# A capacity expert layer inside a scan stage: its steps moved off VectorE and to other slots

## The chip, the cores and the metric

The kernel runs on one core of a Trainium2 chip. A core has five engines, each with its own in-order queue: TensorE (PE; its weight loads are listed as PEld), VectorE (DVE), ScalarE (ACT), GpSimd (POOL) and SyncE (SP), which here only issues transfers. Engines wait for one another by semaphores. The metric is the device time of one execution in microseconds (us); a kernel is judged by the median of several executions.

## The reference

Two blocks are applied to x (32 sequences of 256 tokens of 128 numbers), all in float32. Each block is an attention-like part and a feed-forward part, both with layer norms whose scale, shift and gate come from a small vector per sequence.

- Block 0: an attention over 16 heads of 8, then a mixture of 8 experts of which each token takes 2.
- Block 1, first part: a layer norm, then a Mamba scan forwards and backwards over the tokens (256 channels, 16 states), a norm, and a Fourier layer (sines and cosines of 8 multiples, with a matrix for each).
- Block 1, second part: a mixture of 8 experts in which a token goes to its best expert alone, and each expert takes only its first 80 tokens over the whole batch:

```
expert_idx = argmax(softmax(tokens @ gate_w + gate_b))
pos  = place of the token among those of its expert;  keep = pos < 80
h    = gelu(dispatch @ w1 + b1)                 # 80 x 512 for each expert
out  = (h @ w2 + b2) * gate_prob                # back to the tokens kept
x    = x + gb * out
```

So the last part writes at most 640 of the 8192 rows. The kernel finds them in the first 16 sequences, and only if some expert has not filled its 80 places by then does a branch at the end look at the rest; with these inputs it isn't taken.

## The kernel before

**Stages.** Block 0 runs first, for some 1,450 us. Then comes the scan stage, written in one loop over *units*. A sequence (a "batch" in this text) is 16 units; there are 512. A unit is 1,024 columns of states: PE spreads two vectors over the state rows (`spread_out`, L1447: `arg` and `ub`, both in PSUM), ScalarE takes the exponential (`decay`, L1453), VectorE multiplies `ub` by B (`by_b`, L1464) and scans (`scanned`, L1471), GpSimd multiplies the scan's result by C (`by_c`, L1484), PE sums over the states of two units at once (`gathered`, L1503), and VectorE gates every fourth result (`gate_y`, L1532).

**The order is written by hand.** The loop issues, for iteration g: the spreads of `arg` for unit g+2 and `ub` for g+1, the exponential of g+2, the scan of g, the side steps of slot g, the sum over units g−3 and g−2 (if g is odd), the product by B of g+1, the product by C of g, the gate, and the side steps of slot g+0.5. On PE, ScalarE, VectorE and GpSimd this is the order of the queues. SP's transfers are ordered by when their data and buffers are expected to be ready. `arg` has one PSUM buffer, `ub` two, the scan's result six.

**Side steps** are generators that advance at listed slots, counted from the first unit of their batch. `front(b)` prepares batch b (slots −39 to −3.5: norms, input projections, convolution, the exponential and logarithm of the time steps; its transfers include the load of B and C, `bc`). `gate(b)` takes a silu at −9.5. `back(b)` does the output projection, a norm and the Fourier layer at slots 19 to 44, and for the first 16 batches also the norm ahead of the experts (`last_norm`, 45.5 to 54), which stores the rows, the gates and the shares that the experts read (`fin_d`). Every eight batches `choose` ranks the tokens. In slot p of a batch, steps of three or four batches come together: slot 6.5, say, has the second pair of sines of `back` and the silu of `gate`, slot 3 the first pair and the silu of `front`, slot 12 GpSimd's sums for x, on which VectorE's statistics in slot 12.5 wait.

**One bank.** All side products on PE write one PSUM bank, `m`. A side step that uses it has to wait until the step before has been read.

**Tables.** ScalarE loads a table set before it takes another kind of function. `table(which)` loads it if another is in, and `steps` loads the exponential's set at the end of every call, so after every slot g and every slot g+0.5.

**The experts** of the last part (`expert`, called by `first_places`) run as one stream, one after another, from batch 19 on, each with its weights (`weights_of`: w1, w2, b2, which is broadcast over 128 partitions). Expert e starts in slot 6 of batch 19+e:

- slot 6: the weights' loads, and a gather of the ranks of its places (L1011, an indirect transfer issued by GpSimd)
- 8.5: VectorE compares the ranks with the places (L1022), sums (L1023), and makes the row's number, once as it is for the later scatter (`to_u`) and once limited for the gather (`of_u`; L1024 to L1029)
- 10: the gather of 80 rows of `fin_d` (L1032)
- 13.5: PE transposes them (L1040), VectorE copies the transpose (`dT`, L1042) and multiplies the gate row by the share (L1044)
- 1.5 of the next batch: PE's first product (L1049), gelu on ScalarE (L1055)
- 3.5: PE's second product (L1061), and on VectorE the bias, the product with the gate row, and the sum with x (L1063 to L1065)
- 6: the scatter to the output (L1069)

Each of these tiles has one buffer.

Of the kernel before, what the change touches and what calls it, by code (L numbers as in the profile page):

```python
# [71 lines left out]
def body(ctx: ExitStack, tc: tile.TileContext, a: dict, out: bass.AP):  # L72
# [90 lines left out]
    def over_e(v, n):  # L163
        return v.unsqueeze(2).to_broadcast([P, n, E])
# [737 lines left out]
    chosen = route.tile([P, E, n_t], F32, tag="chosen", name="chosen")  # L902
    rt = pool(ctx, "d_rt")

    def choose(c, bank):

        n = LAST
        restart("d")
        pr = wide(rt, n)
        nc.vector.tensor_tensor(  # L910
            pr[:], lg[:, c % 2 * n : (c % 2 + 1) * n, :], gate_b[:].unsqueeze(1).to_broadcast([P, n, E]), ALU.add
        )
        top = thin(rt, n)
        nc.vector.tensor_reduce(top[:], pr[:], AX.X, ALU.max)
        nc.vector.tensor_tensor(pr[:], pr[:], over_e(top[:], n), ALU.subtract)
        nc.scalar.activation(pr[:], pr[:], AF.Exp)
# [88 lines left out]
        nc.vector.tensor_tensor(at[:], at[:], iota_e[:], ALU.add)  # L1005
        nc.vector.tensor_copy(at_u[:], at[:])

    def expert(pl, e, w1, w2, b2, bank, po_bank, n, table=None, apart=False):

        counts = pl.tile([P, P], F32, tag="counts_of", name="counts_of")  # L1010
        nc.gpsimd.indirect_dma_start(  # L1011
# [5 lines left out]
        yield  # L1017

        token = pl.tile([P, 1], F32, tag="token", name="token")
        to_u = pl.tile([P, 1], U32, tag="to_u", name="to_u")  # L1020
        of_u = pl.tile([P, 1], U32, tag="of_u", name="of_u")
        nc.vector.tensor_scalar(counts[:CAP], counts[:CAP], place[:CAP], None, ALU.is_le)  # L1022
        nc.vector.tensor_reduce(token[:CAP], counts[:CAP], AX.X, ALU.add)  # L1023
        nc.vector.scalar_tensor_tensor(  # L1024
            token[:CAP], in_tile[:CAP, e : e + 1], float(P), token[:CAP], ALU.mult, ALU.add
# [2 lines left out]
        nc.vector.tensor_scalar(token[:CAP], token[:CAP], float(n * P - 1), None, ALU.min)  # L1028
        nc.vector.tensor_copy(of_u[:CAP], token[:CAP])  # L1029
        yield  # L1030
        of = pl.tile([P, FIN], F32, tag="fin", name="fin")[:CAP]
        nc.gpsimd.indirect_dma_start(  # L1032
            out=of,
# [5 lines left out]
        ps = bank()  # L1039
        nc.tensor.transpose(ps[:, :CAP], of[:, 0:D], ident[:CAP, :CAP])  # L1040
        dT = pl.tile([P, CAP], F32, tag="dT", name="dT")
        nc.vector.tensor_copy(dT[:], ps[:, :CAP])  # L1042
        gb = of[:, FIN_G : FIN_G + D]
        nc.vector.tensor_scalar(gb, gb, of[:, FIN_S : FIN_S + 1], None, ALU.mult)  # L1044
        yield
        ph = bank()
        g = pl.tile([P, NF, CAP], F32, tag="g", name="g")
# [8 lines left out]
                g[:, c, :], ph[:, c * P : c * P + CAP], AF.Gelu_apprx_tanh, bias=col("b1", e * NF + c)  # L1056
            )
        yield
        po = po_bank()
        for c in range(NF):  # L1060
            nc.tensor.matmul(po[:CAP, :D], g[:, c, :], w2[:, c, :], start=(c == 0), stop=(c == NF - 1))  # L1061
        y = pl.tile([P, D], F32, tag="y", name="y")[:CAP]
        nc.vector.tensor_tensor(y, po[:CAP, :D], b2[:CAP], ALU.add)  # L1063
        nc.vector.tensor_tensor(y, y, gb, ALU.mult)
        nc.vector.tensor_tensor(y, y, of[:, FIN_X : FIN_X + D], ALU.add)  # L1065
        yield
        if apart:
            nc.gpsimd.memset(apart_of[:], 0.0)
        ins = nc.gpsimd.indirect_dma_start(  # L1069
# [14 lines left out]
    def weights_of(pl, e):  # L1084
# [1 line left out]
        nc.sync.dma_start(w1[:], a["w1_1"][e])  # L1086
        w2 = pl.tile([P, NF, D], F32, tag="w2", name="w2")
        nc.sync.dma_start(w2[:], a["w2_1"][e].rearrange("(c f) d -> f c d", f=P))
        b2 = pl.tile([P, D], F32, tag="b2", name="b2")
        nc.sync.dma_start(b2[:], a["b2"][e].partition_broadcast(P))  # L1090
        return w1, w2, b2

    cont = route.tile([P, E, LAST], F32, tag="cont", name="cont")
# [2 lines left out]
    with ExitStack() as st:  # L1096
# [13 lines left out]
        def bank():  # L1110
            return m_bank
# [24 lines left out]
        def front(b):  # L1136
# [87 lines left out]
            for d in range(2):  # L1224
# [9 lines left out]
                nc.scalar.activation(u[:, d].rearrange("p n t -> p (n t)"), ps[:], AF.Abs)  # L1234
                nc.scalar.activation(dt[:, d].rearrange("p n t -> p (n t)"), ps[:], AF.Relu)
                yield
            nc.scalar.activation(u[:], u[:], AF.Exp, scale=-1.0)
            nc.scalar.activation(u[:], u[:], AF.Ln, bias=1.0)
            yield
# [59 lines left out]
        def back(b, h, ys):  # L1299
# [79 lines left out]
            done = 2 * (b + 1)  # L1379
            if done % LAST == 0:  # L1380
                yield
                yield from choose(done // LAST - 1, bank)
                if b == FIRST - 1:
                    streams.append((b, UNITS * b, first_places(bank), [PLACES_AT] + EXPERTS_AT))

        PLACES_AT = 68
        EXPERTS_AT = [16 * e + at for e in range(4, E + 4) for at in (6, 8.5, 10, 13.5, 17.5, 19.5)]
        EXPERTS_AT.append(16 * (E + 4) + 6)  # L1390


        BACK_AT = (
# [118 lines left out]
        def first_places(bank):  # L1512
# [3 lines left out]
            nc.vector.tensor_reduce(flag[:, 0:1], chosen[0:1, :, n - 1], AX.X, ALU.min)  # L1516
            nc.vector.tensor_scalar(flag[:, 1:2], flag[:, 0:1], float(CAP), None, ALU.is_lt)
            nc.vector.tensor_copy(left[:], flag[:, 1:2])
            yield
            for e in range(E):  # L1520
                yield from expert(few, e, *weights_of(few, e), bank, bank, n, table=table, apart=True)

        gated = {}
        streams = []
# [11 lines left out]
        with tc.manual_schedule(engines=MANUAL):  # L1536
            started = 0

            def steps(at):
                for stream in sorted(streams, key=lambda w: w[0]):  # L1540
                    _, first, work, slots = stream
                    if slots and at == first + slots[0]:
                        slots.pop(0)
                        if next(work, work) is work or not slots:
                            streams.remove(stream)
                if at + 2 < n_u:
                    table(EXP_LN)

            for g in range(FRONT_AT[0], n_u + 6 * UNITS):
# [26 lines left out]
    with tc.If(missing > 0), ExitStack() as st:  # L1576
# [22 lines left out]
                    pass  # L1599
        tile_of_places(wd, n_t)  # L1600
        for e in range(E):
            for _ in expert(sp, e, *weights_of(sp, e), a_bank, a_bank, n_t):
                pass


# [106 lines left out]
```

## Time and profile before

| | |
|---|---|
| median of 5 executions | 3692.46 us (3680.94 to 3700.82) |
| the profiled execution | 3695.73 us, span 3693.9 us |
| first scan starts, last scan ends | 1450.7, 3662.3 us |
| busy: PE, DVE, ACT, POOL | 85%, 71%, 59%, 71% of the span |
| granted PE clock, mean | 0.907 |

"Span" is the time from the first instruction to the last. A group in the profile is all instructions of one line, engine and shape: after the count stand its busy time in us and the mean of one in ns, then the idle time of its engine just before them and what ended it. A line of waits reads: who waited, for whom, us in total, times, the longest. A timeline line has start, duration, engine, source line, operation, and in brackets the idle time before. A line of stretches has, for each stretch of time, its length, then busy us (and instructions) of PE, PEld, DVE, ACT and POOL, the granted clock, the DMA engines' busy share and GB/s. In the slices the span is cut into 40 equal parts, and a digit is the busy share in tenths.

### The profile page before, as it was taken

Reading aid. Unit: us, or ns where it says so; the run is one execution under the profiler, and the core shown is the slowest. Engines: PE = TensorE matmul, PEld = TensorE weight load, DVE = VectorE, ACT = ScalarE, POOL = GpSimd, SP = SyncE. Lnnn points to the kernel's source line nnn. Section 1 sums busy time; section 2 is a strip of 40 time slices with the busy share of each in tenths; the row PEclk is TensorE's granted clock in tenths of the full one; section 3 lists DMA queues with packets and bytes.
Section 4 is the critical chain, followed back from the end, with each engine's and each line's share of the span. In section 5 each row is a group of like instructions: output and inputs, shape, how many; then the busy total and the mean of one; then the engine's idle time right before and its main releaser. Section 6 shows DMA issues by size and latency. Waiting matters only on the chain. (4 is left out here: it accounts for less than half of the span.)

```text
span 3693.9 us, 68522 instructions
## 1 busy us (share of the span) xinstructions
PE 3153.3 (85%) x27356; PEld 2155.2 (58%) x27356; DVE 2621.0 (71%) x3450; ACT 2162.9 (59%) x3242; POOL 2633.4 (71%) x2632
## 2 busy tenths in 40 slices
PE   6989998884999986888889888889888888888886
PEld 3655665552778773555556555556555555555555
DVE  3566666653223223998888888888888888888996
ACT  2666666652223224577676667676666667666775
POOL 4466566555666654888888878888877887778884
PEclk8999999985999996999899889899888899899998
DMA  2630000001222212011121111121111111111100
GB/s 80 266 139 26 24 25 24 26 25 59 91 94 93 67 55 47 21 29 36 32 40 31 32 36 35 33 45 26 32 28 36 34 30 38 38 30 25 28 17 8
DMA packets 133227, 173.73 MB, mean 47 GB/s; under 512 B 26447, under 2 KB 98662, under 8 KB 128676
## 3 DMA queue, kind: packets, MB, share of 16 engines
q1 hardware_dynamic: 105428, 88.13, 10.3%
q0 software_dynamic: 23168, 46.93, 4.0%
q10 hardware_dynamic: 4304, 34.21, 2.3%
q8 instruction: 217, 3.56, 0.4%
q14 instruction: 110, 0.90, 0.1%
HBM read 127.10 MB, written 79.97 MB: 56 GB/s over the span
## 5 line engine op out<-in xcount | busy, mean ns | idle before, releaser
L1484 POOL TENSOR_TENSOR hs<-hs,bc 128x1024 f32<-128x1024 f32 x512 | 1204.8, 2363 | 353.8 <-DVE hs L1471 347.0
L1471 DVE TENSOR_TENSOR_SCAN hs<-da,ub 128x1024 f32<-128x1024 f32 x512 | 1166.5, 2278 | 29.2
L1447 PE MATMUL arg<-dt,spread_a 32*128 32x256 f32 x4096 | 752.9, 436 | 72.8 <-ACT da L1453 71.7
L1453 ACT ACTIVATE da<-arg 128x1020 f32<-128x1020 f32 x512 | 521.7, 1019 | 465.7 <-PE ub L1447 402.3
L1447 PE MATMUL ub<-u,spread 32*128 32x256 f32 x4096 | 652.6, 439 | 92.4 <-DVE hs L1471 45.6
L1464 DVE TENSOR_TENSOR ub<-ub,bc 128x1024 f32<-128x1024 f32 x512 | 620.2, 1211 | 34.6 <-PE ub L1447 34.4
L1447 PEld LDWEIGHTS arg<-dt,spread_a 32*128 32x128 f32 x4096 | 448.8, 201 | 236.9 <-ACT da L1453 126.0
L1447 PEld LDWEIGHTS ub<-u,spread 32*128 32x128 f32 x4096 | 396.5, 204 | 150.8 <-DVE hs L1471 81.0
L578 DVE TENSOR_REDUCE q<-x 128x4 f32<-128x1024 f32 x256 | 312.8, 1222 | 215.3 <-PE x L571 193.3
L571 PE MATMUL e<-qmT,kqT 32*128 32x256 f32 x2048 | 346.9, 416 | 50.5 <-ACT ex L574 45.0
L574 ACT ACTIVATE ex<-e 128x1024 f32<-128x1024 f32 x256 | 261.9, 1023 | 207.3 <-PE x L571 173.6
L1503 PE MATMUL y<-hs,gather 128*32 128x256 f32 x4096 | 333.6, 438 | 6.7 <-POOL hs L1484 6.7
L571 PE MATMUL x<-kqT 32*128 32x256 f32 x2048 | 306.2, 416 | 10.7 <-DVE q L578 10.5
L571 PEld LDWEIGHTS e<-qmT,kqT 32*128 32x128 f32 x2048 | 218.5, 192 | 109.5 <-ACT ex L574 76.6
L1184 PE MATMUL m<-oT,taps 128*128 128x256 f32 (+3 forms) x1024 | 267.7, 407 | 5.9 <-ACT xc L1187 2.0
L1359 PE MATMUL m<-coef,mag 128*128 128x128 f32 x992 | 221.3, 307 | 28.4 <-DVE h L1367 20.7
L1184 PEld LDWEIGHTS m<-oT,taps 128*128 128x128 f32 x1024 | 192.4, 198 | 77.2 <-issue 33.7
L282 POOL DMA_INDIRECT rows_out<-o,to_u x142 | 144.5, 1018 | 109.8 <-ACT o L879 83.1
L1503 PEld LDWEIGHTS y<-hs,gather 128*32 128x32 f32 x4096 | 122.7, 120 | 171.2 <-issue 97.6
L865 DVE TENSOR_TENSOR g<-g,pb 128x512 f32<-128x512 f32 x142 | 97.6, 688 | 173.0 <-PE pb L863 138.2
L1359 PEld LDWEIGHTS m<-coef,mag 128*128 128x128 f32 x992 | 164.6, 208 | 84.4 <-issue 34.9
L1359 PE MATMUL m<-coef,r 128*128 128x128 f32 x992 | 204.7, 290 | 0.0
(348 smaller groups left out, 6109.7 us busy)
## 6 DMA issues: line engine op xcount, KB each, us to landing
rows_in<-blank ACTq DMA_DIRECT2D x4, 8320.0 KB, 25.1
bc_d<-xd SPq DMA_DIRECT2D x64, 256.0 KB, 5.3
bc<-bc_d SPq DMA_DIRECT2D x32, 512.0 KB
of_two<-rows_out SPq DMA_DIRECT2D x64, 128.0 KB, 2.6
mod<-mod SPq DMA_DIRECT2D x32, 192.0 KB, 3.0
x<-in_x SPq DMA_DIRECT2D x16, 256.0 KB, 5.1
mod<-mod SPq DMA_DIRECT2D x32, 128.0 KB, 3.0
w<-in_w SPq DMA_DIRECT2D x16, 256.0 KB
```

Source lines behind the costliest of these rows:

```text
L282: ins = nc.gpsimd.indirect_dma_start(in_offset=None, **args).ins
L571: nc.tensor.matmul(to, lhs, rhs, start=True, stop=True)
L574: nc.scalar.activation(ex[:], exs[k_e][:], AF.Exp, scale=1.0 / math.sqrt(DH))
L578: nc.vector.tensor_reduce(pad("q", b)[:, :, 2 * i : 2 * i + 2, DH].rearrange("p t h -> p h t"), found[:], AX.X, ALU.max, negate=True,)
L1184: nc.tensor.matmul(to, taps[:, d, n, c, :], of, start=(s == 0), stop=(c == 0), skip_group_check=True)
L1359: nc.tensor.matmul(ps[:, t * D : (t + 1) * D], turned[k // (GRID // 2)][1 - j][:, k % (GRID // 2), t * P : (t + 1) * P], coef[:, j, k, :], ...
L1447: nc.tensor.matmul(to, lhs, rhs, start=True, stop=True)
L1453: nc.scalar.activation(e.da.rearrange("p (g t) -> p g t", t=T)[:, :, inner], e.arg[:].rearrange("p i j t -> p (i j) t")[:, :, inner], AF.Exp,)
L1464: nc.vector.tensor_tensor(by_four, by_four, b_of, ALU.mult)
L1471: nc.vector.tensor_tensor_scan(e.hs[:].rearrange("p g t -> p (g t)")[:, ::step], e.da[:, ::step], e.ub[:].rearrange("p i j t -> p (i j t)" ...
L1484: nc.gpsimd.tensor_tensor(e.hs[:], e.hs[:], c_of, ALU.mult)
L1503: nc.tensor.matmul(y[r * RG : (r + 1) * RG, :], gather[:, q, :], of.hs[:, 2 * j + p, :], start=False, stop=(q == NQ - 1), skip_group_check ...
```

## The change

All of it concerns the last experts and ScalarE's tables.

- The compare of ranks goes from VectorE to GpSimd, in a slot of its own. `to_u` and `of_u` get two buffers.
- The copy of the transpose goes from VectorE to ScalarE. VectorE's product of gate row and share is dropped.
- The bias enters the second product as one more matmul with a row of ones (b2 is now one row). ScalarE copies the product out of PSUM, scaled by the share. The product with the gate row and the sum with x go to GpSimd, ahead of the scatter.
- Each expert is a stream of its own, so two are under way at once. With batch 19+e as the start, expert e's slots are: gather of ranks 6.5, compare 10, VectorE's five steps 14.5, weights and gather of rows 15.5; in the next batch transpose and copy 1.5, first product and gelu 6, second product and scaled copy 13.5, GpSimd's two products and the scatter 15.
- The exponential's table set is loaded at the end of a slot g+0.5 only. Where an exponential may come after another set in between, `front` and `choose` ask for the set themselves.

```diff
-    def expert(pl, e, w1, w2, b2, bank, po_bank, n, table=None, apart=False):
+    def expert(pl, e, bank, n, table=None, apart=False):
...
-        to_u = pl.tile([P, 1], U32, tag="to_u", name="to_u")
-        of_u = pl.tile([P, 1], U32, tag="of_u", name="of_u")
-        nc.vector.tensor_scalar(counts[:CAP], counts[:CAP], place[:CAP], None, ALU.is_le)
+        to_u = pl.tile([P, 1], U32, tag="to_u", name="to_u", bufs=2)
+        of_u = pl.tile([P, 1], U32, tag="of_u", name="of_u", bufs=2)
+        nc.gpsimd.tensor_scalar(counts[:CAP], counts[:CAP], place[:CAP], None, ALU.is_le)
+        yield
         nc.vector.tensor_reduce(token[:CAP], counts[:CAP], AX.X, ALU.add)
...
+        w1, w2, b2 = weights_of(pl, e)
         of = pl.tile([P, FIN], F32, tag="fin", name="fin")[:CAP]
...
-        nc.vector.tensor_copy(dT[:], ps[:, :CAP])
-        gb = of[:, FIN_G : FIN_G + D]
-        nc.vector.tensor_scalar(gb, gb, of[:, FIN_S : FIN_S + 1], None, ALU.mult)
+        nc.scalar.copy(dT[:], ps[:, :CAP])
...
-        po = po_bank()
+        po = bank()
+        nc.tensor.matmul(po[:CAP, :D], ones[0:1, :CAP], b2[:], start=True, stop=False)
         for c in range(NF):
-            nc.tensor.matmul(po[:CAP, :D], g[:, c, :], w2[:, c, :], start=(c == 0), stop=(c == NF - 1))
+            nc.tensor.matmul(po[:CAP, :D], g[:, c, :], w2[:, c, :], start=False, stop=(c == NF - 1))
         y = pl.tile([P, D], F32, tag="y", name="y")[:CAP]
-        nc.vector.tensor_tensor(y, po[:CAP, :D], b2[:CAP], ALU.add)
-        nc.vector.tensor_tensor(y, y, gb, ALU.mult)
-        nc.vector.tensor_tensor(y, y, of[:, FIN_X : FIN_X + D], ALU.add)
-        yield
+        nc.scalar.activation(y, po[:CAP, :D], AF.Identity, scale=of[:, FIN_S : FIN_S + 1])
+        yield
+        nc.gpsimd.tensor_tensor(y, y, of[:, FIN_G : FIN_G + D], ALU.mult)
+        nc.gpsimd.tensor_tensor(y, y, of[:, FIN_X : FIN_X + D], ALU.add)
...
-        b2 = pl.tile([P, D], F32, tag="b2", name="b2")
-        nc.sync.dma_start(b2[:], a["b2"][e].partition_broadcast(P))
+        b2 = pl.tile([1, D], F32, tag="b2", name="b2")
+        nc.sync.dma_start(b2[:], a["b2"][e : e + 1])
...
-                    streams.append((b, UNITS * b, first_places(bank), [PLACES_AT] + EXPERTS_AT))
+                    streams.append((b, UNITS * b, first_places(bank), [PLACES_AT]))
...
-        EXPERTS_AT = [16 * e + at for e in range(4, E + 4) for at in (6, 8.5, 10, 13.5, 17.5, 19.5)]
-        EXPERTS_AT.append(16 * (E + 4) + 6)
+        EXPERT_AT = (70.5, 74, 78.5, 79.5, 81.5, 86, 93.5, 95)
...
-            yield
             for e in range(E):
-                yield from expert(few, e, *weights_of(few, e), bank, bank, n, table=table, apart=True)
+                streams.append((n_b, UNITS * (FIRST - 1 + e), first_expert(e, bank), list(EXPERT_AT)))
+            yield
+
+        def first_expert(e, bank):
+            yield from expert(few, e, bank, 2 * FIRST, table=table, apart=True)
...
-                if at + 2 < n_u:
+                if at + 2 < n_u and at % 1:
                     table(EXP_LN)
```

`front` gets a `table(EXP_LN)` ahead of its exponential, and `choose` takes `table` as an argument and loads the exponential's set ahead of its own.

More of the change, by code (lines that the diff above doesn't have):

```diff
@@ L903, in body, with choose @@
     rt = pool(ctx, "d_rt")
-    def choose(c, bank):
+    def choose(c, bank, table=None):
         n = LAST
@@ L915, in choose @@
         nc.vector.tensor_tensor(pr[:], pr[:], over_e(top[:], n), ALU.subtract)
+        if table:
+            table("natural_log_exp_and_others")
         nc.scalar.activation(pr[:], pr[:], AF.Exp)
@@ L1236, in front @@
                 yield
+            table(EXP_LN)
             nc.scalar.activation(u[:], u[:], AF.Exp, scale=-1.0)
@@ L1381, in back @@
                 yield
-                yield from choose(done // LAST - 1, bank)
+                yield from choose(done // LAST - 1, bank, table)
                 if b == FIRST - 1:
-                    streams.append((b, UNITS * b, first_places(bank), [PLACES_AT] + EXPERTS_AT))
+                    streams.append((b, UNITS * b, first_places(bank), [PLACES_AT]))
         PLACES_AT = 68
-        EXPERTS_AT = [16 * e + at for e in range(4, E + 4) for at in (6, 8.5, 10, 13.5, 17.5, 19.5)]
-        EXPERTS_AT.append(16 * (E + 4) + 6)
+        EXPERT_AT = (70.5, 74, 78.5, 79.5, 81.5, 86, 93.5, 95)
         BACK_AT = (
@@ L1518, in first_places @@
             nc.vector.tensor_copy(left[:], flag[:, 1:2])
+            for e in range(E):
+                streams.append((n_b, UNITS * (FIRST - 1 + e), first_expert(e, bank), list(EXPERT_AT)))
             yield
-            for e in range(E):
-                yield from expert(few, e, *weights_of(few, e), bank, bank, n, table=table, apart=True)
+        def first_expert(e, bank):
+            yield from expert(few, e, bank, 2 * FIRST, table=table, apart=True)
         gated = {}
@@ L1601, in body @@
         for e in range(E):
-            for _ in expert(sp, e, *weights_of(sp, e), a_bank, a_bank, n_t):
+            for _ in expert(sp, e, a_bank, n_t):
                 pass
```

## The prediction

> **What bounds the kernel now.** I read the page's slices first, then busy time by stretch, then VectorE's groups and waits among the experts, then timelines of VectorE and GpSimd.
>
> ```profile
> DVE  3566666653223223998888888888888888888996
> ...
> POOL 4466566555666654888888878888877887778884
> PEclk8999999985999996999899889899888899899998
> ```
>
> From slice 16 on runs the scan stage, 512 units. In each, VectorE does the scan (2.28 us) and the product by B (1.21): 3.49 us of the 3.5 to 4 us that most units take, so any step that VectorE does beside them lengthens the run unless VectorE was waiting there anyway. I took the start of every scan (L1471) from the timeline. The gap from scan k to scan k+1 holds what VectorE does in slots k and k+1/2. "Gap p" is the one at unit p of a batch of 16 units:
>
> | batches | 3 | 4 | 7 | 8 | 12 | 13 | 14 | batch in all |
> |---|---|---|---|---|---|---|---|---|
> | 12 to 17 (last norm, no expert) | 3.53 | 5.71 | 6.90 | 3.54 | 6.14 | 3.89 | 3.62 | 68.3 |
> | 20 to 26 (an expert each) | 9.01 | 4.51 | 6.18 | 5.85 | 5.89 | 5.47 | 3.64 | 74.1 |
> | 28 (neither) | 3.53 | 4.73 | 4.26 | 3.53 | 6.15 | 3.48 | 3.65 | 62.5 |
>
> An expert batch costs 11.6 us more than batch 28, in gaps 3, 7, 8 and 13. VectorE's groups between 2750 and 3400 us, then the waits in batches 20 to 26, say why:
>
> ```profile
> L1044 DVE TENSOR_SCALAR fin<-fin 80x128 f32<-80x128 f32 x8 | 16.9, 2116 | 0.0
> ...
> L1022 DVE TENSOR_SCALAR counts_of<-counts_of,place 80x128 f32<-80x128 f32 x8 | 12.4, 1553 | 0.0
> ...
> L1063 DVE TENSOR_TENSOR y<-m,b 80x128 f32<-80x128 f32 x8 | 2.3, 287 | 37.0 <-PE m L1061 23.2 <-ACT xc L1190 13.8
> L1023 DVE TENSOR_REDUCE token<-counts_of 80x1 f32<-80x128 f32 x8 | 2.3, 282 | 0.3
> ...
> L1004 DVE TENSOR_SCALAR at<-in_tile 128x8 f32<-128x8 f32 x1 | 1.8, 1794 | 0.0
> ```
>
> ```profile
> DVE y L1063 <- PE m L1061: 18.6, 4, 4.7
> ...
> DVE y L1063 <- ACT xc L1190: 13.8, 3, 4.6
> ```
>
> L1044 and L1022 take 2.12 and 1.55 us for 128 elements a partition, where the product L1065 of that size takes 0.29: each lasts until the GpSimd product by C that runs beside it ends (L1022 ends 0.08 us after it). They are held. L1063 waits for the second product, which waits in PE's queue for the one m bank: `om` of the backward step sits in it behind two sines on ScalarE.
>
> ```profile
> 3053.58 1.23 DVE L1464 TENSOR_TENSOR ub<-ub,bc 128x1024 f32<-128x1024 f32 x1 [0.78 <-PE ub L1447]
> 3059.47 0.29 DVE L1063 TENSOR_TENSOR y<-m,b 80x128 f32<-80x128 f32 x1 [4.66 <-PE m L1061]
> ```
>
> GpSimd is second. In batch 28 it is busy 55.63 of 62.50 us and late at the batch's end:
>
> ```profile
> 3407.20:3469.70 62.50, 53.88 (x531) 35.67 (x528) 58.67 (x53) 45.91 (x62) 55.63 (x40) 0.99 0.11 23
> ```
>
> ```profile
> 3466.80 4.68 POOL L1484 TENSOR_TENSOR hs<-hs,bc 128x1024 f32<-128x1024 f32 x2
> 3471.57 0.22 POOL L304 TENSOR_SCALAR rstd<-mv 128x2 f32<-128x2 f32 x1
> ...
> 3473.13 2.36 POOL L1484 TENSOR_TENSOR hs<-hs,bc 128x1024 f32<-128x1024 f32 x1
> 3475.44 2.38 POOL L1340 TENSOR_TENSOR r<-r,mag 128x1024 f32<-128x1024 f32 x1
> ```
>
> The product at 3473.13 is unit 15's; its scan ended at 3468.47. GpSimd is 4.7 us late just where the change puts new work.
>
> **Part by part, for each of eight experts.**
>
> *Gap 8: the compare leaves VectorE.* Six steps go: 5.85 − 3.53 = −2.32. GpSimd runs the compare in slot 10, where the gather of rows was (1.03 + 0.16): I take 0.40 from its 128x128 product (0.402), so that slot gets lighter. Nothing paid.
>
> *Gap 13: dT's copy goes to ScalarE, the gate product goes away.* 5.47 − 3.48 = −1.99. Both products, the bias row's and the scaled copy replace them there: PE gets five small matmuls (four took 1.0) for one transpose (0.3). Its queue behind them, the next spread, stands in batch 28 until 3461.38 for a scan anyway; ScalarE is idle there for 3.4 us. Nothing paid; at most 1 us.
>
> *Gaps 3 and 4: the three y steps and their wait go.* 9.01 + 4.51 − 3.53 − 4.73 = −5.26.
>
> *Gap 14: five steps come.* From 3083.12 to 3084.15 in the old place: +1.0. Lower end 0.9 (the durations alone); the upper end is rival C.
>
> *Gap 2: a new wait.* In GpSimd's order, behind the norm's four steps (14.5) now stand two products for y, a memset and the scatter of expert e−1, then C of unit 15, then the gather of e's rows. With the scan of unit 13 as zero, batch 28's rows put unit 15's C at 14.1 to 16.4. New in front: 2 × 0.45, 0.1, 0.26 of gaps, 1.01: 2.3. C ends at 18.75, the gather starts at 18.9. By the trace's DMA records its rows landed 2.46 to 2.62 us after the issue began: 21.5. PE reaches the transpose at 19.9, right after summing units 14 and 15, and stands to 21.5; then 0.4, then the spread of unit 19 (1.5): 23.4. VectorE, moved by +1.0, wants that at 21.0. Stall 2.4. It needs scatter and gather together, so seven times; the last scatter alone makes 1.4 once: 18.2 in all. Lower end 0: the lateness need not build up. Below zero not, since batch 28 has no stall there to lose. Upper end 4: the 1.6 us of lead that I gave VectorE's spread are lost too. I take 2.4: each term is a row next to the place.
>
> *Gap 4:* GpSimd's h rows come later against VectorE, +0.4; 0 to 1.
>
> *Gaps 7 and 8: gelu moves to slot 6.* Its table load (1.28) and four gelus (0.98) now stand ahead of the sines, silu and reload. The reload that used to follow the gelu is gone (eight loads fewer, 10.3 us of ScalarE, which is not the bound). So the exponential of unit 25 ends 2.3 us later. In batch 28 it ended at 3437.79, and the spread behind it at 3437.84 fed a product at 3439.79; 2.3 later costs 1.8. The old expert batches lose 1.9 there too (6.18 against 4.26): a slow PE, and two indirect DMAs on GpSimd in slot 6 where now one stands. I take them as equal: 0. Ends: −1.9 (as batch 28) and +2.3 (the gelu on top).
>
> *The rest.* SP: of the three weight loads, w1 now waits behind xd's two stores for the first product at slot 6, with the next bc load behind it; bc is wanted half a batch later. The bias load shrinks from 128 rows to one. The two index buffers take no time. The exponentials' table is set back after h2T instead of before in batches 0 to 17: the same 1.28 beside a stall that GpSimd's h sets (VectorE waits 1.08 there): 0. The extra load in `choose` falls on a table that is already in: 0.
>
> Removed: 8 × (2.32 + 1.99 + 5.26) = 76.6. Added: 8 × 1.0 + 18.2 + 8 × 0.4 = 29.4. Net −47.2. The profiled execution took 3695.73 (span 3693.9), 3.3 over the median of 3692.46; from the median, **3645**. An expert batch would go from 74.1 to about 68.4.
>
> **A rule of the Trainium skill that speaks against the change.** The page "SBUF — State Buffer", section "Who interferes with whom", says that copies, casts and tensor_scalars on VectorE, and its operations with two SBUF inputs, contend with a GpSimd instruction for a shared port pair, and that the later one blocks until the first is through. The rows above agree for 128 and for 8 elements. By it four of the five steps left on VectorE could each stand behind a product of 2.36, 9.4 per expert, an estimate that would make about 3720 if nothing were given back. Against it: in all eight experts the casts and the tensor_scalar of one element took 0.15 while GpSimd's L305 ran; that was a product of two elements, not of 1024.
>
> **The rivals.**
>
> *B: the new wait doesn't come.* GpSimd catches up, since VectorE pauses elsewhere, and gap 7 falls to batch 28's. For it: batch 28 has the sines and no gap of 6.2. Against: GpSimd's 4.7 us of lag is in that same batch. 3645 − 18 − 3 − 15 = **3609**.
>
> *C: the small steps in gap 14 are held.* For it: L1004, 8 elements, took 1.79 beside a GpSimd product where 0.15 is usual, and in slot 14.5 GpSimd runs products back to back. Three tensor_scalar-like steps × 1.64 = 4.9 per expert; but GpSimd's chain does not move with VectorE, so the 2.4 of gap 2 is given back: +2.5, × 8 = 20: **3665**. Against it: the 0.15 rows beside L305.
>
> *D, the other side: PE's queue stands behind the transpose.* The gather now has two slots until its transpose instead of 3.5, and every spread is behind it. Each microsecond that the rows land later costs one per expert. The change breaks even when a batch loses another 47.2 / 8 = 5.9: rows landing 8.4 us after the issue instead of 2.5. Against: eight landings within 0.2 us of each other. If they took 10: 47 becomes a loss of 12, **3704**.
>
> *E: the clock decides.* Batches 4 to 17 repeat at 68.3 with a slow PE (spread matmuls 0.63 instead of 0.48) in the same two places each time; batch 11, after an interruption, took 64.3. The moved table load could shift that pattern either way: 4 us × 14 = 56 at most, so from 3590 to 3700.
>
> *No effect* is hardly possible: the three held or waiting places are gone from VectorE's order.
>
> **How the numbers follow.** Forecast 0.56 (its own range 3628 to 3662), B 0.16, C 0.18, D 0.05, E 0.05. The range: down to B, with the lower ends 18.2 + 3.2 + 8 × 1.9: 3609; up to C with the gelu on top, 3665 + 8 × 2.3 = 3683. I say 3610 to 3683. A measurement here tells some 0.3% (11 us) from no change. Slower by more: D and a third of E, with what I may have missed, 0.07; within: 0.04; faster 0.89.
>
> **What would show it.** Right: L1022, L1044, L1063 to L1065 gone from VectorE's groups among the experts; gap 3 at 3.5, gap 8 near 3.5 to 5, gap 13 at 3.5; gap 14 at 4.6; gap 2 at about 6, VectorE waiting for PE's ub there; PE waiting at the transpose for the gather; batches 20 to 26 near 68. Wrong: casts of 1.5 us or more in gap 14 (C); gap 2 at 3.65 (B); gap 2 above 9 (D); batches 4 to 17 not at 68.3 (E). Most likely to make it wrong is the sum over gaps 7 and 8, where I set two effects equal, and GpSimd's lag at the batch's end, which one batch without experts supplies.

## The result, and the profile after

The changed kernel takes 3698.63 us (median; 3689.65 to 3710.49) against 3691.43 us of the kernel before on the same chips (3680.59 to 3707.48). The ratio is 1.0021, with a 95% interval of 1.0015 to 1.0027: slower by 0.2%, less than the 0.3% that I took as the smallest change to tell. Forecast were 3645 and a range that ended at 3683. The profiled execution of after, near the upper end of its range, has a span of 3707.6 us, 13.7 over that of before.

The slices of the page after:

```profile
DVE  3566666653223223988888888888888878788996
...
POOL 4466666645666654888888878888877888788884
PEclk6999999985999996898889889989889988888998
```

VectorE has several 8s and 7s late in the scan stage where before it had 8s: it works less. GpSimd and the granted clock look much the same at this scale. Then the batches 20 to 26, from first scan to first scan, as a line of stretches; first before, then after:

```profile
2817.60:3336.50 518.90, 445.15 (x3815) 296.10 (x3807) 446.51 (x441) 348.26 (x470) 410.92 (x302) 0.89 0.14 35
```

```profile
2818.80:3340.10 521.30, 440.38 (x3817) 298.26 (x3813) 421.76 (x399) 341.94 (x476) 420.42 (x319) 0.88 0.14 34
```

VectorE lost 24.8 us of work in seven batches (446.51 to 421.76), 3.5 for each expert, and the stretch is 2.4 us longer. So its idle time grew by 27. Who it waits for there, in the waits of VectorE in that stretch, after:

```profile
DVE ub L1468 <- PE ub L1451: 49.4, 38, 3.3
DVE h L1372 <- PE m L1364: 26.5, 14, 3.3
DVE st L298 <- POOL x L1155: 14.8, 7, 2.1
```

Before, the first of these was 0.8 us in all, the second 19.8 and the third 13.0, with 32.4 for the bank (L1063) beside them. The waits for the bank are gone and waits for PE's spread have come. The groups of VectorE between 2750 and 3400 us, after, say that the steps did leave and that none of the five in gap 14 is held:

```profile
L1468 DVE TENSOR_TENSOR ub<-ub,bc 128x1024 f32<-128x1024 f32 x141 | 171.6, 1217 | 57.0 <-PE ub L1451 56.9
...
L1027 DVE SCALAR_TENSOR_TENSOR token<-in_tile,token 80x1 f32<-80x1 f32 x8 | 2.9, 358 | 0.3
L1026 DVE TENSOR_REDUCE token<-counts_of 80x1 f32<-80x128 f32 x8 | 2.2, 272 | 0.0
...
L1030 DVE CAST to_u<-token 80x1 uint32<-80x1 f32 x8 | 1.2, 150 | 0.3
```

The gaps between scan starts, mean of batches 20 to 26, with the forecast of each below (us; a sum such as 3+4 is of two gaps; gaps 1, 6 and 15 are equal in all):

| gap | 0 | 2 | 3+4 | 5 | 7+8 | 9 | 10 to 12 | 13 | 14 | batch |
|---|---|---|---|---|---|---|---|---|---|---|
| before | 3.55 | 3.65 | 13.52 | 3.48 | 12.03 | 3.84 | 14.25 | 5.47 | 3.64 | 74.1 |
| forecast | 3.55 | 6.05 | 8.66 | 3.48 | 9.71 | 3.84 | 14.25 | 3.48 | 4.64 | 68.4 |
| after | 4.11 | 5.99 | 9.52 | 4.32 | 10.43 | 7.08 | 14.05 | 3.48 | 4.79 | 74.5 |

Gap 2, gap 13 and gap 14 came within 0.15 of the forecast. A batch is 6.1 over the forecast: 3.2 of it in gap 9, 2.3 in gaps 0, 3, 4 and 5 together, 0.7 in gaps 7 and 8 (the other differences come to -0.1). Batches 4 to 17, which have no expert, take 962.4 us in all where they took 962.3.

Gap 2 first, as GpSimd's timeline shows it, with the two lines of PE and VectorE that answer to it:

```profile
3117.25 0.45 POOL L1069 TENSOR_TENSOR y<-y,fin 80x128 f32<-80x128 f32 x1
3117.78 0.45 POOL L1070 TENSOR_TENSOR y<-y,fin 80x128 f32<-80x128 f32 x1
...
3118.58 1.03 POOL L1073 DMA_INDIRECT out<-y,to_u  x1 [0.31 <-POOL apart L1072]
3119.63 2.37 POOL L1488 TENSOR_TENSOR hs<-hs,bc 128x1024 f32<-128x1024 f32 x1
3122.16 0.98 POOL L1036 DMA_INDIRECT fin<-fin_d,of_u  x1 [0.16 <-issue]
```

```profile
3125.08 0.37 PE L1044 MATMUL m<-ident,fin 80*128 80x80 f32 x1 [1.96 <-DMA fin<-fin_d,of_u]
3125.38 0.79 PE L1451 MATMUL arg<-dt,spread_a 32*128 32x256 f32 x1
```

```profile
3127.56 1.23 DVE L1468 TENSOR_TENSOR ub<-ub,bc 128x1024 f32<-128x1024 f32 x1 [2.32 <-PE ub L1451]
```

This is the forecast's chain, step by step: scatter, C of unit 15, gather, and PE at the transpose 2.9 us after the gather's start. But the spread behind the transpose takes 0.79 and 0.63 us a matmul, not the 0.48 and 0.37 of other places: PE was idle for 1.96 us, and the clock fell to half at 3124.51, in that pause.

Slot 6 and what follows it, as timelines of ScalarE, PE and VectorE:

```profile
3145.68 1.28 ACT L1127 ACT_TABLE_LOAD   x1
3146.97 0.98 ACT L1057 ACTIVATE g<-m,cols 128x80 f32<-128x80 f32 x4
3147.97 1.28 ACT L1127 ACT_TABLE_LOAD   x1
3149.26 1.06 ACT L1353 ACTIVATE r<-r 128x1024 f32<-128x1024 f32 x1
3150.23 1.13 ACT L1354 ACTIVATE mag<-mag,halfpi 128x1024 f32<-128x1024 f32 x1
3151.27 0.61 ACT L1252 ACTIVATE sz<-sz 128x512 f32<-128x512 f32 x1
3151.90 1.28 ACT L1127 ACT_TABLE_LOAD   x1
3153.19 1.02 ACT L1457 ACTIVATE da<-arg 128x1020 f32<-128x1020 f32 x1
```

```profile
3148.55 0.49 PE L1364 MATMUL m<-coef,mag 128*128 128x128 f32 x2
3148.88 0.39 PE L1364 MATMUL m<-coef,r 128*128 128x128 f32 x2
...
3154.27 0.48 PE L1451 MATMUL arg<-dt,spread_a 32*128 32x256 f32 x1 [3.66 <-ACT da L1457]
...
3158.78 0.80 PE L1364 MATMUL m<-coef,mag 128*128 128x128 f32 x2
3159.37 0.63 PE L1364 MATMUL m<-coef,r 128*128 128x128 f32 x2
```

```profile
3155.55 1.23 DVE L1468 TENSOR_TENSOR ub<-ub,bc 128x1024 f32<-128x1024 f32 x1 [2.22 <-PE ub L1451]
3156.91 2.29 DVE L1475 TENSOR_TENSOR_SCAN hs<-da,ub 128x1024 f32<-128x1024 f32 x1
3162.48 0.42 DVE L1372 TENSOR_TENSOR h<-h,m 128x256 f32<-128x256 f32 x1 [3.28 <-PE m L1364]
```

The gelu and its table put the exponential at 3153.19. PE's next spread stands behind it for 3.66 us, VectorE waits 2.22 (that is gap 8), and then, about 1 us after PE starts again, the clock halves. The Fourier layer's products (L1364) take 0.80 and 0.63 for what took 0.49 and 0.39 one slot before, and VectorE waits 3.28 for them (gap 9). The trace's clock puts half-clock stretches of 6.8 us at units 2.2 to 2.3, 8.7 and 14.8 to 15.2 in each of batches 22 to 27.

### The profile page after: what moved, and what is told of

Read it like the earlier page. It is cut to its first block, busy times and chain, and to the rows that moved or that the text cites. A ratio compares the mean times of both kernels' runs of the same rounds, so it can differ in the third digit from the quotient of the medians.

```text
span 3707.6 us, 68536 instructions
## 1 busy us (share of the span) xinstructions
PE 3172.7 (86%) x27372; PEld 2176.2 (59%) x27372; DVE 2592.1 (70%) x3402; ACT 2159.2 (58%) x3250; POOL 2649.5 (71%) x2656
## 4 chain that ended last, share of the span: by engine, by line
DVE 19%; PE 17%; POOL 15%; issue 6%; ACT 5%; DMA 1%; DVEq 0%; POOLq 0%; SPq 0%; ACTq 0%
DVE hs L1475 11%; POOL hs L1488 7%; DVE ub L1468 5%; PE arg L1451 4%; PE m L1364 3%; PE y L1507 3%; PE ub L1451 3%; PE m L1188 2%; ACT L1127 2%; POOL dt L1245 2%; ACT da L1457 1%; PE y L1496 1%; POOL r L1345 1%; POOL u L1247 1%; DVE h L1372 1%
## 5 line engine op out<-in xcount | busy, mean ns | idle before, releaser
L1451 PE MATMUL arg<-dt,spread_a 32*128 32x256 f32 x4096 | 744.8, 440 | 82.5 <-ACT da L1457 79.7
L1451 PE MATMUL ub<-u,spread 32*128 32x256 f32 x4096 | 660.9, 442 | 87.5 <-DVE hs L1475 39.1
L574 ACT ACTIVATE ex<-e 128x1024 f32<-128x1024 f32 x256 | 262.1, 1024 | 203.5 <-PE x L571 176.8
L1188 PE MATMUL m<-oT,taps 128*128 128x256 f32 (+3 forms) x1024 | 282.2, 423 | 3.5 <-ACT xc L1191 2.0
L1364 PE MATMUL m<-coef,mag 128*128 128x128 f32 x992 | 227.3, 315 | 29.2 <-DVE h L1372 21.5
L1188 PEld LDWEIGHTS m<-oT,taps 128*128 128x128 f32 x1024 | 201.5, 207 | 79.1 <-issue 40.6
L1364 PEld LDWEIGHTS m<-coef,mag 128*128 128x128 f32 x992 | 169.9, 215 | 86.1 <-DVE h L1372 33.4
L1364 PE MATMUL m<-coef,r 128*128 128x128 f32 x992 | 209.0, 295 | 0.0
## 6 DMA issues: line engine op xcount, KB each, us to landing
rows_in<-blank ACTq DMA_DIRECT2D x4, 8320.0 KB, 24.4
```

Source lines behind the costliest of these rows:

```text
L574: nc.scalar.activation(ex[:], exs[k_e][:], AF.Exp, scale=1.0 / math.sqrt(DH))
L1188: nc.tensor.matmul(to, taps[:, d, n, c, :], of, start=(s == 0), stop=(c == 0), skip_group_check=True)
L1364: nc.tensor.matmul(ps[:, t * D : (t + 1) * D], turned[k // (GRID // 2)][1 - j][:, k % (GRID // 2), t * P : (t + 1) * P], coef[:, j, k, :], ...
L1451: nc.tensor.matmul(to, lhs, rhs, start=True, stop=True)
```

## The experiments

**The theory** after the result: the waits came about as forecast, but each leaves PE idle for some 2 to 4 us, its clock halves, and the next PE work on VectorE's path is late a second time. **Rivals:** the gelu's table alone does it (then gap 9 goes with the table); or the waits alone (then the clock only follows them).

**e1: silu in place of gelu, so no table load of its own.**

```diff
-            table("gelu_apprx_tanh_and_others")
+            table("silu_and_others")
...
-                g[:, c, :], ph[:, c * P : c * P + CAP], AF.Gelu_apprx_tanh, bias=col("b1", e * NF + c)
+                g[:, c, :], ph[:, c * P : c * P + CAP], AF.Silu, bias=col("b1", e * NF + c)
```

> Leaves out: the experts' gelu is computed as a silu, whose table set is the one that the sines behind it need, so one table load (1.28 us) per expert is gone from ScalarE's block in slot 6; nothing else moves. Theory 1 (the block in slot 6 makes the exponential of unit 25 late, PE then idles 3.7 us and its clock falls to half for 6.8 us): PE's idle time falls to about 2.4 us, the half clock behind it does not come, gap 9 falls from 7.1 to 3.9 to 4.3 us and gap 8 from 6.0 to about 4.7; an expert batch goes from 75.0 to about 70.5. Rival (GpSimd's added work sets gaps 8 and 9): both stay within 0.3 us. Gap 2 stays near 6.0 in either.

Measured in one execution: 3686.68 us (before, on the same chip: 3695.24). Gap 8 fell to 4.39, as foretold. Gap 9 did not follow: 6.78. The timelines of PE and VectorE at that place:

```profile
2993.36 0.48 PE L1451 MATMUL arg<-dt,spread_a 32*128 32x256 f32 x1 [2.23 <-ACT da L1457]
...
2995.63 0.56 PE L1451 MATMUL arg<-dt,spread_a 32*128 32x256 f32 x1 [0.28 <-ACT da L1457]
...
2995.99 0.63 PE L1451 MATMUL arg<-dt,spread_a 32*128 32x256 f32 x1
```

```profile
2994.60 1.23 DVE L1468 TENSOR_TENSOR ub<-ub,bc 128x1024 f32<-128x1024 f32 x1 [0.75 <-PE ub L1451]
...
3000.48 0.42 DVE L1372 TENSOR_TENSOR h<-h,m 128x256 f32<-128x256 f32 x1 [2.23 <-PE m L1364]
```

The stall of gap 8 is down to 0.75, so the load made most of it. PE still idles for 2.23 us, and from 2.3 us after it resumes it runs slow. The first rival falls: less lateness did not restore the clock, though I had expected that it would.

**e2: six small matmuls on PE in slot 7.5** (128 x 256, a result that nobody reads), the lateness left as it is. They begin a sum of their own in the bank that holds the running sum of y, so the kernel's values differ; the order of the other steps doesn't.

```diff
+        if apart:
+            for _ in range(6):
+                nc.tensor.matmul(idle_bank, idle_w[:, :P], idle_w[:, :T], start=True, stop=True, skip_group_check=True)
+            yield
         po = bank()
...
-        EXPERT_AT = (70.5, 74, 78.5, 79.5, 81.5, 86, 93.5, 95)
+        EXPERT_AT = (70.5, 74, 78.5, 79.5, 81.5, 86, 87.5, 93.5, 95)
```

> Adds six matmuls (128x256, of constants, into an unused half of a bank) per expert on PE, in slot 7.5 behind the Fourier products, where PE idles 3.7 us; nothing reads them. Theory 1, its clock half: PE's idle time falls to 1 to 1.5 us, the clock stays full, gap 9 falls from 7.1 to about 3.9 us though PE does more, while gap 8 stays at 5.8 to 6.0, since the exponential is as late as before; an expert batch goes from 75.0 to about 72. Rival (gap 9 is a wait for the bank or for GpSimd, and the slow matmuls only come with it): gap 9 stays at 7 or grows.

Measured in one execution: 3662.95. Gap 8 is still 5.83, and gap 9 is 4.57. The stretch of batches 20 to 26:

```profile
2799.60:3298.40 498.80, 425.13 (x3921) 287.79 (x3917) 421.29 (x399) 342.17 (x477) 420.54 (x319) 0.96 0.15 35
```

More PE instructions, 22.5 us less time, a clock of 0.96 where it was 0.88; none of these batches has a half-clock stretch at units 8 to 9, where all of after's have one. The second rival falls too: with the exponential as late as before, work for PE in its pause takes the second stall away. This is the run that decides on gap 9.

**e3: the first product and gelu go to slot 13.5,** the second product to 14.5, where no sines stand behind them.

```diff
-        EXPERT_AT = (70.5, 74, 78.5, 79.5, 81.5, 86, 93.5, 95)
+        EXPERT_AT = (70.5, 74, 78.5, 79.5, 81.5, 93.5, 94.5, 95)
```

> First product and gelu move from slot 6 to 13.5 (where ScalarE idles 3.4 us in batch 28), second product to 14.5; one table load more per expert. Theory 1: gap 8 back to 3.5, gap 9 to 3.85, gaps 13 to 0 together at most 1.5 us longer; an expert batch from 75.0 to 69 to 70, the kernel some 40 us faster than the changed one (about 3658). Rival (gaps 8 and 9 are GpSimd's): they stay at 6.0 and 7.1, and the kernel gets no faster.

Measured: 3660.41, ratio to before 0.991 (0.9894 to 0.9927). Gap 8 is 3.65. Gap 9 is 5.66 in the mean, two batches at 4.3 and 4.6 and five at 6.1 to 6.2. These five have half clock for 3.4 us at unit 8.9 to 9.0, the two have none. That the sines alone leave PE idle long enough for it is a reading. Batches 20 to 26 take 491.2.

**e4: the scatter goes to slot 6.5 of the batch after,** so the gather of the next rows no longer stands behind it; the rows get a second buffer for that.

```diff
-        of = pl.tile([P, FIN], F32, tag="fin", name="fin")[:CAP]
+        of = pl.tile([P, FIN], F32, tag="fin", name="fin", bufs=2)[:CAP]
...
-        EXPERT_AT = (70.5, 74, 78.5, 79.5, 81.5, 86, 93.5, 95)
+        EXPERT_AT = (70.5, 74, 78.5, 79.5, 81.5, 86, 93.5, 102.5)
```

> GpSimd's two products for y and the scatter move from slot 15 to slot 6.5 of the next batch (the rows' tile gets two buffers); all else as in the changed kernel. Theory 2 (gap 2 is the transpose waiting for rows whose gather stands on GpSimd behind the scatter and unit 15's product by C): the gather is issued 2.3 us earlier against VectorE, gap 2 falls from 6.0 to 3.7 to 4.2 us, gap 8 and 9 stay or grow a little; an expert batch about 2 us shorter, the kernel about 15 us faster than the changed one. Rival (gap 2 is set by PE's own slow clock at the batch's end): gap 2 stays within 0.5 us.

Measured: 3664.91, ratio 0.993 (0.9905 to 0.9956). Gap 2 fell from 5.99 to 3.78: the scatter and its two products in GpSimd's queue are what made VectorE wait there. PE still stands for the rows at the transpose (13.2 us in batches 20 to 26, where after has 13.7), but now early enough for VectorE. Gaps 8 and 9 keep 6.35 and 6.84.

**e5: the engines of the change, the slots of before:** held steps on GpSimd and ScalarE, products in their old places.

```diff
-        EXPERT_AT = (70.5, 74, 78.5, 79.5, 81.5, 86, 93.5, 95)
+        EXPERT_AT = (70, 72.5, 73.5, 74, 77.5, 81.5, 83.5, 86)
```

> The steps stay on the engines that the change gave them, but go back to the old places of the batch: gather of ranks 6, compare 8.5, VectorE's five steps 9.5, gather of rows 10, transpose 13.5, first product and gelu 1.5, second product and scaled copy 3.5, GpSimd's products and scatter 6. It tells the two halves of the change apart. Theory (the engines' half is worth what was forecast, and the loss came from the slots): gap 8 from 5.85 to 3.5, gap 9 from 3.84 to about 5, gap 13 from 5.47 to 3.5, gap 3 falls, but PE's second product still waits for the one bank and the spread stands behind it, so gaps 3 and 4 fall only from 13.5 to 11 to 12; no stall in gap 2, gaps 7 to 9 without the gelu in front; an expert batch from 74.1 to 69 to 70.5, the kernel near 3660. Rival (GpSimd's added work costs wherever it stands): 74 or more, the kernel not faster than before.

Measured: 3646.39, against 3678.17 of before on that chip; ratio 0.9911 (0.9891 to 0.9931). So moving the steps off VectorE is worth 0.9% by itself, and the change's slots lose all of it. Gap 8 is 3.53 and gap 13 3.48 (both as the forecast had them); gaps 3 and 4 give only 1.3, since PE's second product now stands for the bank in gap 4, up to 1.4 us (for `om` on ScalarE). And gap 9 is 6.37, in part for a reason I had not looked for. VectorE's timeline at that place, with GpSimd's product beside it:

```profile
2986.57 1.83 DVE L1027 SCALAR_TENSOR_TENSOR token<-in_tile,token 80x1 f32<-80x1 f32 x1
2988.43 0.15 DVE L1030 CAST to_u<-token 80x1 uint32<-80x1 f32 x1
2988.62 0.15 DVE L1031 TENSOR_SCALAR token<-token 80x1 f32<-80x1 f32 x1
```

```profile
2986.04 2.34 POOL L1488 TENSOR_TENSOR hs<-hs,bc 128x1024 f32<-128x1024 f32 x1
```

The one-element step with two inputs lasts until GpSimd's product ends, at 2988.4.

**e6: both moves, e3 and e4 together.**

```diff
-        of = pl.tile([P, FIN], F32, tag="fin", name="fin")[:CAP]
+        of = pl.tile([P, FIN], F32, tag="fin", name="fin", bufs=2)[:CAP]
...
-        EXPERT_AT = (70.5, 74, 78.5, 79.5, 81.5, 86, 93.5, 95)
+        EXPERT_AT = (70.5, 74, 78.5, 79.5, 81.5, 93.5, 94.5, 102.5)
```

> Both moves together: gelu in 13.5 with the second product in 14.5, and GpSimd's y products and scatter in 6.5 of the next batch. Theories 1 and 2 add: gap 2 at 3.7 to 4.2 (6.0 in the changed kernel), gap 8 at 3.6 (6.0), gap 9 at 3.9 to 5.7 (7.1); an expert batch from 75 to about 67.5, the kernel near 3642. Rival (the clock makes one loss out of both, so that they don't add): no better than 3655.

Measured: 3632.18, ratio 0.9872 (0.9843 to 0.99), 46 us under before on that chip. Batches 20 to 26 take 471.9, with 44.4 us at half clock where after has 123.5. Gap 9 is still 5.38, gap 3 4.30 and gap 5 4.29.

**e7: as e6, and VectorE's five steps (and the compare) earlier,** away from GpSimd's late products at the batch's end.

```diff
-        EXPERT_AT = (70.5, 74, 78.5, 79.5, 81.5, 93.5, 94.5, 102.5)
+        EXPERT_AT = (70.5, 74, 76, 79.5, 81.5, 93.5, 94.5, 102.5)
```

> As with both moves, and VectorE's five steps go from slot 14.5 to slot 12, ahead of the statistics, for which VectorE waits 2.1 us (GpSimd's x). Expected: gap 14 from 4.8 to 3.65, gap 12 unchanged at 6.15 (the steps fill the wait) or 0.3 longer; an expert batch another 1.1 us shorter, the kernel 9 us faster than with both moves. Rival (GpSimd's lateness just moves on): gap 12 unchanged, but gaps 0 to 2 give the 1.1 us back.

Measured: 3631.36, ratio 0.9875 (0.9833 to 0.9917): nothing beyond e6. Gap 14 fell by 1.1 to 3.68, and gap 2 rose by 1.0 to 5.10: VectorE came earlier to the rows that it waits for. L1027 took 0.71 there, in the mean of its group.

**e8: as e7, and small matmuls on PE in six places of a batch,** as many as given (before slot p's steps, before and after those of slot p+0.5; slots 1 and 7 only beside experts).

```diff
+        def kept_busy(at, where):
+            b, p = divmod(at, UNITS)
+            if not 0 <= at < n_u - UNITS:
+                return
+            n = where.get(p, 0)
+            if p in (1, 7) and not FIRST + 4 <= b < FIRST + 4 + E:
+                n = 0
+            for _ in range(n):
+                nc.tensor.matmul(y_bank[:, 1, :], in_w[:, :P], in_w[:, :T], start=False, stop=False, skip_group_check=True)
+
+        BEFORE, HALF, AFTER = {4: 2}, {1: 3, 3: 3}, {7: 3, 13: 2, 14: 4}
...
+                kept_busy(g, BEFORE)
                 steps(g)
...
+                kept_busy(g, HALF)
                 steps(g + 0.5)
+                kept_busy(g, AFTER)
```

> As the one with the five steps in slot 12, and matmuls of constants that nothing reads (128x256, added onto an unused half of a bank) on PE where it idles: in every batch two in 4, three in 3.5, two in 13.5, four in 14.5, and in the expert batches three in 1.5 and three in 7.5. If PE's idling is what lowers its clock, and the lowered clock sets the 68.3 us of batches 4 to 17: those batches fall to 64.5 to 66 us, the expert batches to about 65, the kernel to 3580 to 3610. Rival (the slow matmuls are off the path, or the clock falls for another reason): batches 4 to 17 stay at 68.3, and the kernel is as fast as without or slower by the extra matmuls.

Measured: 3594.17, ratio 0.9779 (0.975 to 0.9809), 84 us under the kernel before on that chip. The slices of the clock, and batches 20 to 26:

```profile
PEclk8999999986899997999999999999999999999998
```

```profile
2780.20:3240.80 460.60, 431.99 (x4071) 299.41 (x4067) 423.14 (x400) 350.41 (x484) 420.34 (x319) 1.00 0.16 38
```

Clock 1.00, 3.4 us at half clock in 460.6; gaps 0, 2, 3 and 5 at 3.51, 3.65, 3.53 and 3.59. PE does more and all is faster. Batches 4 to 17 fell from 962.4 to 949.0, 1.0 a batch, where I had expected 2.3 to 3.8. In gap 15 the added matmuls cost 1.5.

**e9: the change as it stood, with e8's matmuls and nothing else** (the edit is the last one, on the changed kernel).

> The changed kernel, slots and buffers untouched, with the same small extra matmuls on TensorE as in e8 (a result nobody reads, in seven places of a batch), so that TensorE does not idle there. It tells the clock's part of the loss from that of the waits. Theory (the late exponential of slot 6 and the rows' wait of gap 2 are there by themselves, and the falls of the clock that they set off make the rest): gaps 0, 3 and 5 of batches 20 to 26 go back to 3.5, 3.5 to 4.3 and 3.5 to 3.6, gap 9 to 4.6 or less, while gap 2 stays at 5.5 to 6 and gap 8 at 5.5 to 6; the extra matmuls themselves cost up to 1.6 in gap 15 as in e8; an expert batch 70 to 72, the run 3630 to 3650. Rival (the clock only follows the waits): gap 9 stays near 7 and gap 3 near 4.6; an expert batch 74 to 76, the run about 3670.

Measured: 3660.37, against 3678.41 of before; ratio 0.995 (0.9937 to 0.9963), and slower than the 3630 to 3650 that I had expected. Gaps 0, 3 and 5 went to 3.57, 3.53 and 3.59 (from 4.11, 4.65 and 4.32), while gaps 2 and 8 stayed at 6.07 and 6.08. So those three were the clock's: it is 0.95 in these batches, where after has 0.88. Gap 9 stayed at 6.47, where I had expected 4.6: three matmuls in slot 7.5 did not do what e2's six did. PE's timeline:

```profile
3035.16 0.48 PE L1463 MATMUL arg<-dt,spread_a 32*128 32x256 f32 x1 [2.37 <-ACT da L1469]
```

Still 2.37 us idle, as in e1, and the clock still fell at unit 8.5 to 8.9.

**e10: the kernel before with the same matmuls,** meant as the other half of e9.

> The kernel before with the same extra matmuls in the same places. With e9 it compares the change at a clock that is mended in both. The prediction's sum by itself (47 less) should show again in e9 against e10 if it failed by the clock alone; if slot 6 fails too, by 2.3 to 2.5 in each of eight batches, 27 to 29 are left. Rival (the change is worth nothing at any clock): e9 and e10 within 10. I expect 3660 to 3675 here, about 25 over e9, gap 3 still at 8 to 9 by the wait for the bank, gap 8 at 5.85 and gap 13 at 5.5 (these are not the clock's), batches 4 to 17 at 67 to 68 in the mean as in e8.

Measured: 3701.32, ratio 1.0059 (1.0037 to 1.0082): slower, where I had expected 3660 to 3675. The waits of VectorE in its batches 20 to 26:

```profile
DVE y L1063 <- PE m L1061: 33.5, 7, 4.8
DVE ub L1476 <- PE ub L1459: 31.6, 14, 3.6
```

The second line is new. The four matmuls after slot 14 write the bank that VectorE's gate reads; PE stands 3.68 us for the gate there, behind VectorE's held L1044, and gap 15 is 7.15. Its batches 20 to 26 still have 95.6 us at half clock, where before has 110.6 and e9 47.8. So e10 is no clean control: its 41 us over e9 can't be read as the change's worth at a mended clock. That stays open.

**e11: e8 without the four matmuls after slot 14;** in their place one group of the convolution in slot 14.5 is done twice.

```diff
-        BEFORE, HALF, AFTER = {4: 2}, {1: 3, 3: 3}, {7: 3, 13: 2, 14: 4}
+        BEFORE, HALF, AFTER = {4: 2}, {1: 3, 3: 3}, {7: 3, 13: 2}
...
-                    for c in range(DC - 1, -1, -1):
+                    again = 2 if (d, n) == (0, 1) else 1
+                    for c in [*range(DC - 1, -1, -1)] * again:
```

> e8 without the four extra matmuls at the end of slot 14; in their place the convolution's group of four matmuls in slot 14.5 is done twice, in the bank that it has anyway. In e8 the four waited in TensorE's queue for VectorE's gate (2.3 idle in one batch of three, then half clock), and gap 15 took 4.6 to 6.2 instead of 3.5. If that wait was the cause, gap 15 goes to 3.5 to 3.8 and the run to 3555 to 3570; if the extra matmuls there were what kept the clock up, the half clock at unit 15 comes back in batches 4 to 17 (gap 0 at 4.9) and the run is at 3600 or above.

Measured: 3608.02, ratio 0.9812 (0.9792 to 0.9832). Gap 15 did go to 3.5 in batches 3 to 17 (but for batch 10), so the wait for the gate was its cause; but in batches 4 to 17 half clock came at units 1.9 to 2.3 (in seven of the 14; in e8 in none) and stayed at 6.4 to 7.1 (in ten; in e8 in nine). Gap 4, which was 4.7 to 6.4 in e8, rose to 6.1 to 7.4 but for batch 11. What was won in one gap was lost in the others. e8 stays the fastest of all.

## Why the prediction was wrong

**Right, with their sizes:** gap 8's six steps off VectorE (e5 shows 3.53 without the gelu), gap 13 (3.48), the new wait in gap 2 (2.34 a batch, forecast 2.4, and e4 takes it away by moving the scatter), gap 14 (+1.15, forecast +1.0). The bank's wait is gone. In gap 2 the chain was right: the gather starts 19.0 us after unit 13's scan, forecast 18.9. That the stall's size agrees is in part luck. In five of the seven batches VectorE could go on at some 22.1 and not at 21.0, and the spread that it waits for, at half clock, came at 24.4 and not at 23.4; the two differences cancel.

Rival B did not come, since the new wait did. Nor did D: PE had the rows 2.9 us after the gather's start in each of the eight batches. C did not come either, and the timelines of VectorE and GpSimd in gap 14 of after show how near it was:

```profile
3110.61 0.36 DVE L1027 SCALAR_TENSOR_TENSOR token<-in_tile,token 80x1 f32<-80x1 f32 x1
3111.01 0.15 DVE L1030 CAST to_u<-token 80x1 uint32<-80x1 f32 x1
3111.19 0.15 DVE L1031 TENSOR_SCALAR token<-token 80x1 f32<-80x1 f32 x1
```

```profile
3108.61 2.35 POOL L1247 TENSOR_TENSOR u<-dt,xc 128x1024 f32<-128x1024 f32 x1
3110.92 4.67 POOL L1488 TENSOR_TENSOR hs<-hs,bc 128x1024 f32<-128x1024 f32 x2
```

L1027 ends with GpSimd's product, at 3110.97: it was held, but only for the product's last part. The cast and the tensor_scalar run beside the next product and take 0.15: steps of one element of that kind are not held.

**The step that failed** is "Gaps 7 and 8: gelu moves to slot 6 … I take them as equal: 0". For those two gaps it was off by 0.7 only: gap 7 won 1.8, gap 8 is 2.5 over the 3.53. I had the 2.3 by which the exponential is later. What I left out is what it does to PE: idle for 3.66 us, half clock, and gap 9, +3.2, a gap for which the sum has no term. Of those 3.2 e2 gives back 2.5 with nothing but work for PE in the pause. So the move of the gelu, priced at 0, measured 4.0 a batch (0.7 and 3.2, rounded).

**The second part of the miss** is rival E, which asked the clock only for batches 4 to 17, where nothing moved (962.4 against 962.3). In the expert batches each of the two new waits of VectorE for PE was also a new pause of PE. Gap 2's 1.96 us of it is followed by half clock at unit 2.3. Gaps 0, 3, 4 and 5 lose 2.3 a batch over the forecast; e9 wins 0.5, 1.1 and 0.7 in gaps 0, 3 and 5 by added matmuls alone. (Gap 4 rose by 0.85 in e9; two of the added matmuls stand ahead of slot 4's steps.)

So of the 6.1 that an expert batch lies over the forecast, some 4.0 came away by added PE work alone, and so were the clock's: 2.5 in gap 9 by e2, and by e9 1.2 in gaps 0 and 5 and 0.3 in gaps 3 and 4 together. These are two runs; none has both. Some 0.7 each are the gelu's in gaps 7 and 8 and what e2 leaves in gap 9, and 0.6 is left in gaps 3 and 4. The total of half-clock time in batches 20 to 26 rose little, from 110.6 to 123.5 us. It moved: before, it lay mostly about units 3.2, 5.6 to 6.2, 10 and 14.8, the first of these (in four of the seven batches) in the gap in which VectorE waited some 4.6 us for the bank anyway. That a part of it was hidden there is how I read the places; no run separates it.

## What to carry to other kernels

Price a wait on a busy TensorE twice: the time that it stands, and the half-speed work behind it. Before a step is moved, list the pauses of PE that the new order makes, the short ones too, and see what PE does in the next 7 us and who waits for it. Where pauses can't be avoided, a few matmuls that nobody needs can be worth their time (e2, e8), but they must not wait for anybody themselves (e10).

## What the runs showed of the hardware

- The clock changed in steps of 3.41 us; in the scan stage of after, 62 of 79 stretches at half clock lasted 6.83 us and 15 lasted 3.41. There, the 3.41 us before a fall had PE busy 0.50 of the time in the median (worked out from PE's rows), 3.41 us that kept the clock 0.98. It is no sharp threshold: 0.48 kept it once, and some of 0.82 lost it. Pauses of 1.96 us (gap 2), 2.23 (e1) and 2.37 (e9) were each followed by half clock. In batches 20 to 26 of before no pause of PE is over 2.15 us, and 110.6 us are at half clock; in e8 none is over 1.22, and 3.4 us are.
- The page "TensorE: Matmul & The Clock Gate" of the Trainium skill, section "HAM oscillation — how this bites in real kernels", gives the rule as no idle gaps of PE over some 3.4 us. By it e1, e9 and the kernel before would have kept their clock there; the measured pauses of 2.23, 2.37 and 2.15 say that in a stream of short waits less is enough.
- The expert batches of after settle at 75.0 us and batches 12 to 17 of before at 68.3 (of after 68.2 in the mean), within 0.1 of 22 and 20 times 3.413: a batch that sets off its own falls of the clock repeats in step with it. That the step forces these lengths is a reading, not shown.
- The same one-element step with two inputs (L1027) took 0.36 us in after, 0.71 in e7 and 1.83 in e5: in all eight experts of each it ended some 0.02 us after the GpSimd product that had begun before it, so its time is that product's remainder. Casts and tensor_scalars of one element took 0.15 in each of these, in after beside a product of 1024 elements. The page "SBUF — State Buffer" of the Trainium skill, section "Who interferes with whom", has operations with two SBUF inputs contend with a GpSimd instruction that reads, and names casts and tensor_scalars among those that can, on conditions for their operands; here the first agrees, and the second did not occur for one element a partition.
